# Row edges as corrections beside a convolution over all columns, and loads of X in three pairs

## The chip, the cores and the metric

The kernel runs on one core of a Trainium2 chip. The metric is device time in microseconds from the start to the end of one execution. Engines are named as the profile names them: PE multiplies matrices, PEld loads its weights, DVE and POOL work on elements, ACT scales and copies, SP issues most DMAs. Each engine works through its own queue in order and waits for the others by semaphores.

## The reference, cut to what matters

Four modulated convolutions run one after the other over rows of 1024 samples with 64 channels, for 128 batch rows, and their result is added to the input:

```python
TYPES = ('same', 'upsample', 'same', 'downsample')      # K = 3 taps, 64 -> 64 channels
def _layer(x, style, w, b, mw, mb, typ):
    s = style @ mw.T + mb
    weight = SCALE * w * s[:, None, :, None]
    demod = lax.rsqrt(jnp.sum(weight * weight, axis=(2, 3)) + EPS)
    weight = weight * demod[:, :, None, None]
    if typ == 'same':
        out = jax.vmap(_conv_same)(x, weight) + b[None, :, None]
    elif typ == 'upsample':
        out = _blur(jax.vmap(_conv_up)(x, weight.transpose(0, 2, 1, 3)) + b[None, :, None], 2.0 * blur_k, (1, 1))
    elif typ == 'downsample':
        out = jax.vmap(_conv_down)(_blur(x, blur_k, (2, 2)), weight) + b[None, :, None]
    return out
out = x
for i, typ in enumerate(TYPES):
    out = _layer(out, style, weights[i], biases[i], mod_w[i], mod_b[i], typ)
return x + out
```

Nothing in it is nonlinear in x, so away from the ends of a row the four layers are a single convolution with nine taps and a weight matrix of its own for each batch row. Near the ends, up to three outputs a side, every layer pads with zeros and cuts off what it computes beyond the row, and there the nine taps alone don't give the result.

## The kernel before, in words

The kernel works on groups of four batch rows, q = 0 to 31; two rows lie in the two halves of the 128 partitions (64 channels each), two more in a second plane. A matmul uses a 64 by 64 quadrant of PE, and four of them belong together (two halves in, two halves out). For each group a chain on PE builds the nine taps (`stage1_a`, `stage1_b`, `stage2`, `stage3_b`, `stage3_a`), while the input is turned into five sums and differences of shifted thirds of a row (`in04`, `in1`, `in2`, `in3`, `in_g01`, `in_g2`: DVE and POOL read X, write G, then T). Then five products of three matmul groups each (`conv0` to `conv4`, all in `product`, L803), over NB = 340 columns, give three interleaved planes of outputs, which ACT scales and biases into a tile `o` (`output`, L880) and SP stores (`store`, L885).

The order is written out by hand. `early_turn(q)` runs for q = 0 to 3, `turn_of(q)` for 4 to 28, and the code behind it does the last three groups. A turn finishes group q, convolves group n = q + 1, builds the taps of c = q + 2 and starts those of s = q + 4. X has two buffers. In a turn the loads of group c + 1 are issued together behind `r_sums(c)`: three planes with two DMAs each. SP issues DMAs in the order of the code, so stores and loads queue behind one another.

The ends are a second, small computation for all 128 rows at once. It takes eight input columns at each end (`x_ends` into Xe), runs all four layers on them (`ends0`, `ends1` in two parts, `ends2`, `ends3`, all through `ends_matmul`, L1044) with scalings and blurs between (`rest0` to `rest3`, `add0`, `add2`, `blur_side`), adds bias and input (`rest3_bias`) and stores three finished outputs per end (`out_ends`). Its matmul groups stand in turns 10, 14, 15 and 19 (the table SLOTS) ahead of `conv1`, in the two PSUM banks of Y, and `ends3` in turn 28 in a bank pair psE of its own. The table SIDE gives DVE one small piece of it in most turns from 8 to 27. The big convolution skips the three columns at each end, and the host puts the parts together.

Of the kernel before, what the change touches and what calls it, by code (L numbers as in the profile page):

```python
# [63 lines left out]
def kernel(  # L64
# [74 lines left out]
    Xs = [const.tile([P, 2, NXC], F32, name=f"X{i}") for i in range(NX)]  # L139
# [24 lines left out]
    Xe = const.tile([P, B, 8], F32, name="Xe")  # L164
# [9 lines left out]
    NB = 340  # L174
# [578 lines left out]
    def g_tile(q):  # L753
        if q not in Gs:
            Gs[q] = gpool.tile([P, 2, 3 * PL], F32, tag="G", name=f"G{q}")
        return Xs[q % NX], Gs[q]
# [6 lines left out]
    def in_g01(q, pairs=BOTH_PAIRS):  # L763
        if q < NQ:
            X, g = g_tile(q)
            sum_of(g[:, pairs, PL:], X[:, pairs, : 2 * PL], 0.5, X[:, pairs, PL:], ALU.subtract)
# [126 lines left out]
    WIDE = 6  # L893
    ends_ps = {}

    def slot(matmuls, n, ps, wide=WIDE):
        matmuls(ps)
        ends_ps[0] = ps, max(n, wide)

    def last(i, n, j):  # L900
        ps, w = ends_ps[0]
        return ps[i][:, : n * w].rearrange("c (b j) -> c b j", b=n)[:, :, :j]


# [81 lines left out]
    Xm = const.tile([P, B, 8], F32, name="Xm")  # L986
    Xs0 = [Xm[:, :HB], Xm[:, HB:]]
    a0, c0, a2, c2 = (const.tile([P, HB], F32, name=n) for n in ("a0", "c0", "a2", "c2"))
    g1 = const.tile([P, 6, C], F32, name="g1")

    Ye = [const.tile([P, HB, 8], F32, name=f"Ye{s}") for s in range(2)]
    Ue = [const.tile([P, HB, 11], F32, name=f"Ue{s}") for s in range(2)]
    Ve = [const.tile([P, HB, 12], F32, name=f"Ve{s}") for s in range(2)]
    Oe = const.tile([P, B, 3], F32, name="Oe")

    def zeros():
        for t in Ye:
            nc_g.memset(t[:, :, 0:1], 0.0)
            nc_g.memset(t[:, :, 7:8], 0.0)
        for t in Ue:  # L1000
            nc_g.memset(t[:, :, 0:1], 0.0)
            nc_g.memset(t[:, :, 10:11], 0.0)
        for t in Ve:
            nc_g.memset(t[:, :, 0:2], 0.0)
            nc_g.memset(t[:, :, 10:12], 0.0)
        nc_g.memset(g1, 0.0)

    def spread(t, n):

        return t[:, :, None].to_broadcast([P, t.shape[1], n])  # L1010
# [7 lines left out]
    def setup_x(h):  # L1018
        bs = slice(h * HB, (h + 1) * HB)
        nc_v.tensor_tensor(Xm[:, bs], Xe[:, bs], spread(sc[:, 0, bs], 8), op=ALU.mult)  # L1020

    def setup0():

        for rows, bs in ((T, slice(0, HB)), (Bo, slice(HB, B))):
            nc_v.tensor_mul(a0[rows], dm[rows, 1, bs], dm[rows, 0, bs])
            nc_v.tensor_copy(c0[rows], c0f[rows, bs])
# [4 lines left out]
    def setup3():  # L1031
        for rows, bs in ((T, slice(0, HB)), (Bo, slice(HB, B))):
            nc_v.tensor_copy(a2[rows], Da[rows, bs])
            nc_v.tensor_copy(c2[rows], c2f[rows, bs])

    def ends_matmul(ps, n, taps, weight, moving, wide=WIDE):
        for i in reversed(range(taps)):
            first = i == taps - 1
            w = max(n, wide)
            m = w if first else n  # L1040
            for r, rows in enumerate(HALF):
                for c, cols in enumerate(HALF):
                    dst = ps[r][cols, : HB * w].rearrange("c (b j) -> c b j", j=w)
                    nc.tensor.matmul(  # L1044
                        dst[:, :, :m],
                        weight(i, r, c)[rows],
                        moving(i, r, c, m)[rows],
                        start=first,
                        stop=(i == 0),
                        skip_group_check=True,  # L1050
                    )

    def ends0(ps):

        ends_matmul(
            ps, 6, K, lambda i, r, c: wio[0][:, i, :], lambda i, r, c, m: Xs0[c][:, :, i : i + m]
        )

    def rest0():
        for s in range(2):  # L1060
            dst = Ye[s][:, :, 1:7]
            nc_v.tensor_tensor(dst, last(s, HB, 6), spread(a0, 6), op=ALU.mult)

    def add0(s):
        dst = Ye[s][:, :, 1:7]
        nc_v.tensor_tensor(dst, dst, spread(c0, 6), op=ALU.add)

    def ends1(part):

        n = 5 - part  # L1070


        def weight(i, r, c):
            return g1[:, 2 * i + (part if c == 0 else 1 - part), :]

        def moving(i, r, c, m):
            col = 2 - i + (c + part if c else 0)
            return Ye[c][:, :, col : col + m]

        return lambda ps: ends_matmul(ps, n, K, weight, moving)  # L1080

    def rest1(part):
        n = 5 - part
        for h in range(2):
            bs = slice(h * HB, (h + 1) * HB)
            dst = Ue[h][:, :, 1 + part : 10 : 2]
            nc_v.tensor_tensor(dst, last(h, HB, n), spread(a1[:, bs], n), op=ALU.mult)

    def rest1_bias(h):

        bs = slice(h * HB, (h + 1) * HB)
        dst = Ue[h][:, :, 1:10]
        nc_v.scalar_tensor_tensor(
            dst, spread(b1s[:, bs], 9), 2.0, dst, op0=ALU.mult, op1=ALU.add
        )

    def rest1_edges(h):

        bs = slice(h * HB, (h + 1) * HB)
        for rows, col in ((T, 1), (Bo, 9)):  # L1100
            dst = Ue[h][rows, :, col]
            nc_v.scalar_tensor_tensor(
                dst, b1s[rows, bs], -0.25, dst, op0=ALU.mult, op1=ALU.add
            )

    def ends2(ps):

        ends_matmul(
            ps,
            8,  # L1110
            K,
            lambda i, r, c: wio[2][:, i, :],
            lambda i, r, c, m: Ue[c][:, :, i + r : i + r + m],
        )

    def rest2():
        for s in range(2):
            dst = Ve[s][:, :, 2:10]
            nc_v.tensor_tensor(dst, last(s, HB, 8), spread(a2, 8), op=ALU.mult)

    def add2(s):
        dst = Ve[s][:, :, 2:10]
        nc_v.tensor_tensor(dst, dst, spread(c2, 8), op=ALU.add)


    def blur_side(s, part):
        at = (2 * s, 0, 0)[part]
        src = (Ve[s], Ue[s], Ve[s])[part][:, :, at : at + 10 - part]
        dst = (Ue[s], Ve[s], Ue[s])[part][:, :, : 9 - part]
        nc_v.tensor_tensor(dst, src[:, :, :-1], src[:, :, 1:], op=ALU.add)  # L1130

    def ends3(ps):

        ends_matmul(
            ps,
            3,
            K,
            lambda i, r, c: wio[3][:, i, :],
            lambda i, r, c, m: Ue[c][:, :, i : i + 5 : 2],
            wide=3,  # L1140
        )

    def rest3():
        for h in range(2):
            bs = slice(h * HB, (h + 1) * HB)
            nc_v.scalar_tensor_tensor(
                Oe[:, bs],
                last(h, HB, 3),
                0.125,
# [572 lines left out]
```

## Time and profile before

| what | value |
|---|---|
| median of 3 runs | 475.82 us (474.04 to 476.01) |
| the profiled execution, its span | 475.5 us; no other time of it is recorded |
| DVE busy | 417.3 us |
| ACT busy | 312.0 us |
| POOL busy | 165.8 us |
| bytes read from and written to HBM | 35.36 MB, 33.62 MB |

Busy times are those of one execution, engine by engine; they overlap. In a row of the profile stand a line of the code, the engine, the operation, the tiles written and read, a form, and how often it occurred; behind it the time busy in all, the mean length of one in ns, and the idle time of the engine just before it with what ended that. Rows of the time order have start and length in us. A matmul of FP32 stands twice in the profile, once per pass.

### The profile page before, as it was taken

Reading aid. Unit: us, or ns where it says so; the run is one execution under the profiler, and the core shown is the slowest. Engines: PE = TensorE matmul, PEld = TensorE weight load, DVE = VectorE, ACT = ScalarE, POOL = GpSimd, SP = SyncE. Lnnn points to the kernel's source line nnn. Section 1 sums busy time; section 2 is a strip of 40 time slices with the busy share of each in tenths; the row PEclk is TensorE's granted clock in tenths of the full one; section 3 lists DMA queues with packets and bytes.
Section 4 is the critical chain, followed back from the end, with each engine's and each line's share of the span. In section 5 each row is a group of like instructions: output and inputs, shape, how many; then the busy total and the mean of one; then the engine's idle time right before and its main releaser. Section 6 shows DMA issues by size and latency. Waiting matters only on the chain.

```text
span 475.5 us, 26771 instructions
## 1 busy us (share of the span) xinstructions
PE 469.7 (99%) x11932; PEld 349.5 (74%) x11932; DVE 417.3 (88%) x694; ACT 312.0 (66%) x711; POOL 165.8 (35%) x200
## 2 busy tenths in 40 slices
PE   9999999999999999999999999999999999999996
PEld 6987788777678876677776677766788787876653
DVE  3889998879989998899979899979998999999896
ACT  4565657577766676766667666667666777766464
POOL 3634033664444342233432233422333423243200
PEclk9999999999999999999999999999999999999999
DMA  5237456535445554345544454543555544455225
GB/s 176 71 115 224 150 151 180 152 113 177 139 145 166 166 166 136 123 150 169 163 150 126 130 168 152 178 124 121 152 164 169 164 145 147 148 152 161 80 91 193
DMA packets 52707, 70.71 MB, mean 149 GB/s; under 512 B 6000, under 2 KB 50672, under 8 KB 52592
## 3 DMA queue, kind: packets, MB, share of 16 engines
q1 hardware_dynamic: 52368, 68.78, 46.3%
q8 instruction: 93, 1.52, 1.4%
q10 hardware_dynamic: 224, 0.22, 0.1%
q14 instruction: 22, 0.18, 0.1%
HBM read 35.36 MB, written 33.62 MB: 145 GB/s over the span
## 4 chain that ended last, share of the span: by engine, by line
PE 99%; DVE 0%; ACT 0%; issue 0%
PE psA L803 47%; PE Y L803 12%; PE psR L506 9%; PE psW L621 7%; PE psA L621 7%; PE psS L428 6%; PE psR L589 5%; PE psA L506 2%; PE Y L1044 2%; PE Y L183 1%; PE Y L379 1%; PE psM L220 0%; PE psE L1044 0%; PE Y L255 0%; DVE o L882 0%; PE psM L255 0%
## 5 line engine op out<-in xcount | busy, mean ns | idle before, releaser
L803 PE MATMUL psA<-T,H 64*64 64x340 f32 x2304 | 185.9, 446 | 0.0
L803 PEld LDWEIGHTS psA<-T,H 64*64 64x64 f32 x2304 | 90.7, 133 | 46.9 <-issue 2.5
L712 DVE SCALAR_TENSOR_TENSOR G<-X 128x1376 f32<-128x1376 f32 (+2 forms) x65 | 78.0, 1206 | 0.2
L776 POOL TENSOR_TENSOR T<-G 128x684 f32<-128x684 f32 x28 | 46.3, 1652 | 73.7 <-DVE G L712 73.7
L484 POOL TENSOR_TENSOR S<-S 128x128 f32<-128x128 f32 x28 | 21.6, 772 | 139.7 <-ACT S L399 139.6
L399 ACT ACTIVATE R<-psR,tC 128x448 f32<-128x448 f32 x63 | 36.6, 631 | 43.6 <-PE psR L506 25.8
L803 PE MATMUL psA<-T,Wf 64*64 64x340 f32 x768 | 63.7, 446 | 0.0
L803 PE MATMUL Y<-T,Wf 64*64 64x340 f32 x768 | 62.4, 451 | 0.0
L712 DVE SCALAR_TENSOR_TENSOR Y<-m,psA 128x340 f32<-128x340 f32 x62 | 32.0, 516 | 28.2 <-PE psA L803 26.9
L399 ACT ACTIVATE psW<-psA 128x128 f32<-128x128 f32 x100 | 19.3, 268 | 49.1 <-PE psA L621 45.0
L790 DVE TENSOR_TENSOR T<-G 128x1368 f32<-128x1368 f32 (+1 forms) x33 | 50.8, 1541 | 0.0
L399 ACT ACTIVATE Wf<-psW,t 128x256 f32<-128x256 f32 (+2 forms) x76 | 32.7, 480 | 26.7 <-PE psW L621 26.4
L761 DVE TENSOR_TENSOR T<-X 128x684 f32<-128x684 f32 x32 | 47.7, 1492 | 0.0
L506 PE MATMUL psR<-S,E 64*64 64x64 f32 (+1 forms) x1472 | 46.8, 237 | 0.0
L781 POOL TENSOR_TENSOR T<-G 128x684 f32<-128x684 f32 x28 | 46.5, 1660 | 0.0
L428 PEld LDWEIGHTS psS<-wd,w2n 64*64 64x64 f32 x1120 | 35.1, 133 | 12.9 <-issue 0.3
L506 PEld LDWEIGHTS psR<-S,E 64*64 64x64 f32 x1472 | 39.5, 134 | 4.9 <-ACT psR L529 0.2
L803 PEld LDWEIGHTS Y<-T,Wf 64*64 64x64 f32 x768 | 30.3, 132 | 16.8
L803 PEld LDWEIGHTS psA<-T,Wf 64*64 64x64 f32 x768 | 29.8, 133 | 14.5
L880 ACT ACTIVATE o<-psA,tb,td 128x340 f32<-128x340 f32 x63 | 37.1, 648 | 5.0 <-PE psA L803 2.8
L880 ACT ACTIVATE o<-y,tb,td 128x340 f32<-128x340 f32 x62 | 38.5, 678 | 0.0
L880 ACT ACTIVATE o<-Y,tb,td 128x340 f32<-128x340 f32 x62 | 36.1, 639 | 2.8 <-PE Y L803 2.0
(180 smaller groups left out, 840.4 us busy)
## 6 DMA issues: line engine op xcount, KB each, us to landing
out<-o SPq DMA_DIRECT2D x191, 170.0 KB, 2.6
X<-in_x SPq DMA_DIRECT2D x150, 172.0 KB, 3.4
X<-in_x SPq DMA_DIRECT2D x14, 516.0 KB, 5.0
par<-in_params SPq DMA_DIRECT2D x3, 192.0 KB, 3.8
Xe<-in_x_ends SPq DMA_DIRECT2D x1, 512.0 KB, 4.5
out<-Oe SPq DMA_DIRECT2D x2, 96.0 KB, 2.1
out<-o ACTq DMA_DIRECT2D x1, 170.0 KB, 2.8
par<-in_params SPq DMA_DIRECT2D x1, 160.0 KB, 2.7
```

Source lines behind the costliest of these rows:

```text
L399: nc_a.activation(dst, src, AF.Copy, scale=f)
L428: nc.tensor.matmul(ps[r][cols, at * C : (at + n) * C], weight[rows], wd[c if r == 0 else 1 - c][rows, taps], start=first, stop=last, skip_ ...
L506: nc.tensor.matmul(dst[r][cols], weight[rows], st[c if r == 0 else 1 - c][rows, slots, :], start=False, stop=last, skip_group_check=True,)
L589: nc.tensor.matmul(ps[r][cols, lo * C : (lo + m) * C], E[rows, e + 2, :], src[rows, a, :], start=(n == 0), stop=(n == 8), skip_group_check ...
L621: nc.tensor.matmul(dst[r][cols], weight[rows], t[rows, c, slots, :], start=first, stop=last, skip_group_check=True,)
L712: nc_v.scalar_tensor_tensor(out, x, f, y, op0=ALU.mult, op1=op)
L761: nc_v.tensor_sub(t[:, pairs, 0, :NJ], plane(X, 3, pairs), plane(X, 1, pairs))
L776: eng.tensor_add(t[:, :, 0, :NJ], plane(g, 2), plane(g, 1))
L781: eng.tensor_sub(t[:, :, 1, :NJ], plane(g, 2), plane(g, 1))
L790: nc_v.tensor_sub(t[:, pairs, :, :NJ], both(a, PL), both(b, 1))
L803: nc.tensor.matmul(ps[s][cols, :NB], w, Ts[q, tag][rows, c, i, g : g + NB], start=(g == 0 and (m == 3 or alone)), stop=(g == K - 1), skip_ ...
L880: nc_a.activation(dst, src, AF.Identity, bias=add, scale=d3)
```

## The change

Four things are changed, and they hang together.

The big convolution now computes every column: the host pads each row with four zeros instead of one, NB grows from 340 to 342, and the buffers of X and G get eight more columns, which are set to zero once for X. Outputs 0 to 1023 of a row all come out of it, the three at either end as if no layer had cut anything off.

The computation of the ends gives only what those outputs have too much. It needs three input columns per end instead of eight, and fewer columns in each layer: per end 3, then 6, 5 and 3. Both ends share tiles (a second index instead of two tiles), the right end mirrored, so that one operation serves both. `ends_matmul` now takes a plan of (weight, columns read, columns written), many of them with steps of 2 to 6 elements.

The edges are corrected on the chip. `gather(q - 1)` copies the six edge outputs of a finished group from `o` into Oc on POOL, in two small operations per turn. In turn 28 one DVE operation subtracts the corrections Oe from those of 27 groups, and one DMA stores them; the last five groups are subtracted one by one, on POOL and at the very end on DVE, and a last DMA stores them. The tables that the ends need (`end_tables`) are made on POOL in turns 8 to 10.

The places move. The end matmuls write the psA banks of the group before and stand between `stage2` and `conv2`, in turns 11, 15, 19 and 27. The loads of X are issued as three pairs: behind `r_sums`, behind the stores of the third outputs, and behind those of the second outputs.

```diff
-    Xs = [const.tile([P, 2, NXC], F32, name=f"X{i}") for i in range(NX)]
+    Xs = [const.tile([P, 2, NXC + 8], F32, name=f"X{i}") for i in range(NX)]
+    for t in Xs:
+        nc_g.memset(t[:, :, NXC:], 0.0)
...
-    NB = 340
+    NB = 342
...
+    def ends_matmul(ps, n, moving, plan):
+        for i, (weight, src, dst) in enumerate(plan):
             for r, rows in enumerate(HALF):
                 for c, cols in enumerate(HALF):
+                    out_ = ps[r][cols, : HB * n].rearrange("c (b j) -> c b j", j=n)
+                    d = dst(r) if callable(dst) else dst
                     nc.tensor.matmul(
+                        out_[:, :, d],
+                        weight(r, c)[rows],
+                        moving[rows, c, :, src],
...
     def ends0(ps):
+            Xm,
+            (
+                (w[2], slice(0, 3), slice(0, 3)),
+                (w[1], slice(0, 2), slice(1, 3)),
+                (w[0], slice(0, 1), slice(2, 3)),
+            ),
...
+    def ends1(ps):
+            Ye,
+            (
+                (g[0], slice(2, 4), slice(1, 6, 4)),
+                (g[2], slice(1, 3), slice(1, 6, 4)),
+                (g[1], slice(1, 3), slice(0, 3, 2)),
+                (g[4], slice(0, 2), slice(3, 6, 2)),
+                (g[3], slice(1, 2), slice(2, 3)),
+                (g[5], slice(0, 1), slice(4, 5)),
+            ),
...
+    def ends2(ps):
+            Ue,
+            (
+                (w[0], slice(0, 5), slice(0, 5)),
+                (w[1], slice(1, 5), slice(0, 4)),
+                (w[2], slice(2, 5, 2), slice(0, 3, 2)),
+                (w[2], slice(5, 6), slice(1, 2)),
+            ),
...
     def ends3(ps):
+            We,
+            (
+                (w[0], slice(0, 3, 2), lambda r: slice(0, 2 + r, 1 + r)),
+                (w[0], slice(4, 5), lambda r: slice(2 - r, 3 - r)),
+                (w[1], slice(1, 4, 2), lambda r: slice(0, 2 + r, 1 + r)),
+                (w[2], slice(2, 5, 2), lambda r: slice(0, 2 + r, 1 + r)),
             ),
...
+    def correct(q, planes, eng=nc_g):
+        src, b = edges(q, planes)
+        at = slice(b, b + 2)
+        if q < LATER_ENDS:
+            eng.tensor_copy(Oc[:, at, :, planes], src)
+        else:
+            eng.tensor_sub(Oc[:, at, :, planes], src, Oe[:, at, :, planes])
+
+    def gather(q):
+        for planes in (slice(1, K), slice(0, 1)):
+            correct(q, planes)
...
-    SLOTS = {
-        10: (ends0, 6, rest0),
-        14: (ends1(0), 5, lambda: rest1(0)),
-        15: (ends1(1), 4, lambda: rest1(1)),
-        19: (ends2, 8, rest2),
-    }
+    SLOTS = {10: (ends0, rest0), 14: (ends1, rest1), 18: (ends2, rest2), 26: (ends3, rest3)}
...
     def turn_of(q):
...
+            if q - 1 in SLOTS:
+                SLOTS[q - 1][0](banks(q - 1))
             conv2(q)
             r_sums(c, nc_g)
+            if q - 1 in SLOTS:
+                SLOTS[q - 1][1](A[q - 1])
             sum2(q)
             in2(n, nc_g)
         side(TABLES, q)
-        for i in range(3):
-            load(c + 1, slice(i, i + 1))
+        load(c + 1, slice(0, 1))
...
         outputs(q, 2)
+        load(c + 1, slice(1, 2))
...
         outputs(q, 1)
+        load(c + 1, slice(2, 3))
...
         outputs(q, 0)
-        if q in SLOTS:
-            matmuls, width, rest = SLOTS[q]
-            slot(matmuls, width, Y_banks)
-            rest()
-        if s == NQ:
-            slot(ends3, 3, unit(ps_w, "psE"), 3)
-            rest3()
...
         in3(c)
+        gather(q - 1)
...
+    correct(q, slice(1, K), nc_v)
     conv0(q, *range(K))
     for i, (eng, queue) in enumerate(zip(BOTH, (nc_a, nc.sync))):
         output(q, 0, i, eng)
         store(q, i, slice(0, 1), queue)
+    correct(q, slice(0, 1), nc_v)
+    store_ends(LATER_ENDS, NQ)
```

On PE, the first end convolution stood at the end of turn 10 before, between the shared taps (L506, writing psA) and `conv1` of group 11 (L803); behind it stage 2 begins (psR):

```order
L506 MATMUL psA_3057<-S_3164,E 64x64 x12
L1044 MATMUL Y<-Xm,par 64x384 x12
L803 MATMUL psA_3327<-T_11_3239,H_3059 64x340 x12
L506 MATMUL psR_0_3488<-S_3164,E 64x2x64 x2
L506 MATMUL psR_1_3489<-S_3164,E 64x2x64 x2
```

Now it stands in turn 11, between the last rows of stage 2 (psR) and `conv2` of group 11, ahead of stage 3 (L623); the third number of a form is what lies together in a step:

```order
L508 MATMUL psR_0_3508<-S_3180,E 64x64 x2
L508 MATMUL psR_1_3509<-S_3180,E 64x64 x2
L1042 MATMUL psA_3071<-Xm,par 64x192 x4
L1042 MATMUL psA_3071<-Xm,par 64x64x2 x4
L1042 MATMUL psA_3071<-Xm,par 64x64 x4
L807 MATMUL psA_3347<-T_11_3259,H_3073 64x342 x12
L623 MATMUL psA_3631<-R_3596,w0s_154 64x192 x4
```

It has moved past `conv1` and stage 2, and has three shapes of falling size where it had one.

On POOL, a turn held four operations before: a sum into S (L484), a sum into T (`in1`, L776), a sum into R (L638) and a difference into T (`in2`, L781):

```order
L484 TENSOR_TENSOR S_3164<-S_3164 128x2x64
L776 TENSOR_TENSOR T_11_3239<-G_3172 128x2x342
L638 TENSOR_TENSOR R_3301<-R_3301 128x2x128
L781 TENSOR_TENSOR T_11_3239<-G_3172 128x2x342
L484 TENSOR_TENSOR S_3434<-S_3434 128x2x64
```

Now the two copies of `gather` stand between the first two; this turn is one of the three that also make tables (c1h, Dar and c2r), at its end:

```order
L486 TENSOR_TENSOR S_3180<-S_3180 128x2x64
L1166 COPY Oc<-o_2884 128x4x2
L1166 COPY Oc<-o_2884 128x4
L780 TENSOR_TENSOR T_11_3259<-G_3188 128x2x344
L640 TENSOR_TENSOR R_3321<-R_3321 128x2x128
L785 TENSOR_TENSOR T_11_3259<-G_3188 128x2x344
L334 TENSOR_SCALAR c1h<-cc_151 64x64 x2
L1021 COPY Dar<-Da 128x128
L1022 COPY c2r<-c2f 128x128
```

So L776, now L780, has two more operations ahead of it on its engine, and the next sum into S has the tables ahead of it in turns 8 to 10.

On SP, two turns read like this before, six loads and six stores in turn:

```order
L146 DMA X_105<-in_x 128x344 x6
L885 DMA out<-o_4798 128x340 x6
L146 DMA X_106<-in_x 128x344 x6
L885 DMA out<-o_5085 128x340 x6
L146 DMA X_105<-in_x 128x344 x6
```

Now one turn and the start of the next read:

```order
L889 DMA out<-o_4833 128x342 x2
L148 DMA X_105<-in_x 128x344 x2
L889 DMA out<-o_4833 128x342 x2
L148 DMA X_105<-in_x 128x344 x2
L889 DMA out<-o_4833 128x342 x2
L148 DMA X_106<-in_x 128x344 x2
L889 DMA out<-o_5105 128x342 x2
```

The second and third pair have moved behind two and four stores of the same turn.

282 lines of the change are left out of this document (127 added, 155 removed).

## The prediction

> **What bounds the kernel now.** I read the page first, then the chain of work that ended last in order of time, then the engines' sums in one turn, then the list of waits. The page:
>
> ```profile
> span 475.5 us, 26771 instructions
> ...
> PE 469.7 (99%) x11932; PEld 349.5 (74%) x11932; DVE 417.3 (88%) x694; ACT 312.0 (66%) x711; POOL 165.8 (35%) x200
> ```
>
> PE is busy for 469.7 of 475.5 us. A busy PE need not be a fast one, so I look at what it does per turn (one pass of the loop over groups of four batch rows), in the chain that ended last (start, length, engine, tile, line) and in the sums of one turn (columns of the second fence: stretch, its length, then busy time of PE, PEld, DVE, ACT, POOL, clock, DMA share, GB/s; the first number of an engine is its time).
>
> ```profile
> 187.59 1.94 PE psR L506 x112
> 189.53 1.72 PE psA L803 x24
> ...
> 201.44 1.94 PE psR L506 x112
> ```
>
> ```profile
> 201.20:215.05 13.85, 13.85 (x388) 9.79 (x384) 12.74 (x20) 9.80 (x24) 4.81 (x4) 1.00 0.49 155
> ```
>
> The chain is PE's own work. One product (12 matmuls, 24 passes) takes 1.72 us, and stage 2 comes round again after 201.44 - 187.59 = 13.85 us, all of it PE busy at the full clock. An end convolution (L1044) is one more link: it makes its turn longer by all it costs. DVE is next with 12.74 of 13.85 us, so it has 1.11 us to spare per turn, and the waits say the same:
>
> ```profile
> DVE Y L712 <- PE psA L803: 26.9, 26, 1.9
> ```
>
> DVE waits for PE 26 times, 1.0 us each: PE sets the turn, with little room above DVE. So I price PE first, and then ask whether anything new reaches DVE's 1.1 us.
>
> **Part 1: the end convolutions that go.** Each group stands between the start of its first matmul and the start of PE's next product (PE alone, in order of time):
>
> ```profile
> 183.76 2.12 PE L1044 MATMUL Y<-Xm,par 64*64 64x384 f32 x24
> 185.70 0.74 PE L803 MATMUL psA<-T,H 64*64 64x340 f32 x6
> ```
> ```profile
> 241.06 1.92 PE L1044 MATMUL Y<-Ye,g 64*64 64x384 f32 x24
> 242.79 0.47 PE L803 MATMUL psA<-T,H 64*64 64x340 f32 x4
> ```
> ```profile
> 256.63 1.81 PE L1044 MATMUL Y<-Ye,g 64*64 64x384 f32 x24
> 258.25 0.76 PE L803 MATMUL psA<-T,H 64*64 64x340 f32 x8
> ```
> ```profile
> 313.75 2.78 PE L1044 MATMUL Y<-Ue,par 64*64 64x512 f32 x24
> 316.35 1.03 PE L803 MATMUL psA<-T,H 64*64 64x340 f32 x12
> ```
> ```profile
> 440.35 1.58 PE L1044 MATMUL psE<-Ue,par 64*64 64x192 f32 x24
> 441.75 1.04 PE L803 MATMUL psA<-T,H 64*64 64x340 f32 x12
> ```
>
> 1.94 + 1.73 + 1.62 + 2.60 + 1.40 = **9.29 us** leave PE.
>
> **Part 2: those that come.** Four quadrants run at once (24 passes of 446 ns, part 3, end in 1.72 us), so I count sets of four passes: 1.72 us / 6 sets / 340 columns = 0.843 ns a column. ends2 has the same rate (2.60 us / 6 / 512 = 0.846). The new plans hold, per quadrant, 192 + 128 + 64 = 384 columns (ends0), 4x128 + 2x64 = 640 (ends1), 320 + 256 + 128 + 64 = 768 (ends2) and 128 + 64 + 2x128 = 448 (ends3): 2240, where the old had 5184. At 0.843 ns and two passes that is 3.78 us. But most read or write every second, third or sixth element. The nearest row is ends3 of before, which reads every second element: 1.40 us / 6 / 192 = 1.215 ns, 1.44 times as much. I take 0.843 ns for the 768 columns of the matmuls that write and read runs of three or more (192, 320 and 256) and 1.215 ns for the other 1472: 1.29 + 3.58 = **4.9 us**. No row shows a write to PSUM that skips single elements. Bounds: 3.8 us if skipping is free, and 6.4 us if a skipping write costs the 1.44 once more (1.75 ns). Below 3.8 it can't go, since even dense columns take that.
>
> [...] The rows here show a skipping read, and no skipping write.
>
> **Part 3: two more columns in every product.**
>
> ```profile
> L803 PE MATMUL psA<-T,H 64*64 64x340 f32 x2304 | 185.9, 446 | 0.0
> ...
> L803 PE MATMUL psA<-T,Wf 64*64 64x340 f32 x768 | 63.7, 446 | 0.0
> L803 PE MATMUL Y<-T,Wf 64*64 64x340 f32 x768 | 62.4, 451 | 0.0
> ```
>
> 3840 passes are 160 products. Each grows by 6 sets x 2 columns x 0.843 ns = 10.1 ns, together **+1.6 us**. DVE's and ACT's rows grow by 2 in 340 as well: 12.74 us by at most 0.6% is 0.07 us of DVE's 1.11.
>
> **Part 4: the copies and corrections of the edges.** POOL now makes two small copies a turn between L484 and the sum at L776, 8 and 4 elements a partition. Small POOL operations and the idle time before L776:
>
> ```profile
> 33.69 0.23 POOL L934 TENSOR_TENSOR c2f<-sc,par_s 128x16 f32<-128x16 f32 x1
> ...
> 43.41 1.64 POOL L930 TENSOR_TENSOR Da<-sc,dm 128x16 f32<-128x16 f32 x1
> ```
> ```profile
> L776 POOL TENSOR_TENSOR T<-G 128x684 f32<-128x684 f32 x28 | 46.3, 1652 | 73.7 <-DVE G L712 73.7
> ```
>
> So a copy costs 0.23 to 1.64 us; I take 0.23, the row that is nearest in size (16 elements a partition). Two are 0.46 us, inside the 73.7 / 28 = 2.6 us that POOL sits idle there: **0**. Queued behind them is L776 (into conv1 almost a turn later). If the cover is gone, DVE pays; that is the second rival. The twelve POOL operations of end_tables in turns 8 to 10 fall in L484's idle time in the same way, and the two pads of X stand at the start, ahead of a wait.
>
> **Part 5: the new places.** The end matmuls now write psA of the turn before and stand ahead of conv2. The scaling on DVE must be done before stage 3 reopens that bank, one product (1.72 us) later; behind it on DVE stands sum2, which waits for conv2 there anyway (the 1.0 us above). So nothing is late: **0**. In turn 28 DVE gets one more operation, of 324 elements, and SP the store of its result ahead of two row stores: about 0.5 us of DVE's 1.1, **0** too. The side work on DVE shrinks (its rows have 3 to 6 elements per edge, where they had 8).
>
> **Part 6: the loads of X.**
>
> ```profile
> 211.86 0.87 DVE L712 SCALAR_TENSOR_TENSOR G<-X 128x684 f32<-128x684 f32 x1
> ...
> 212.63 1.25 ACT L880 ACTIVATE o<-y,tb,td 128x340 f32<-128x340 f32 x2
> ```
> ```profile
> DMA to landing us min/median/max: 2.4/4.2/4.4
> ```
>
> (The second fence is the landings of the loads in two turns.) The last pair now queues on SP behind the second outputs, which end at 213.9; with two issues of 0.4 us it lands by 219.2. Its first reader is the row at 211.86, one turn on: 225.7. 6.5 us to spare, so **0**; if that cover went, DVE would pay each us. Stores behind a load wait no longer than they did: a load issues at once when its buffer is free, and X's readers finish a turn earlier.
>
> **Part 7: the end.**
>
> ```profile
> 471.00 0.63 ACT L880 ACTIVATE o<-psA,tb,td 128x340 f32<-128x340 f32 x1 [2.28 <-DMA out<-o]
> 471.06 0.63 DVE L882 TENSOR_SCALAR o<-psA,td,tb 128x340 f32<-128x340 f32 x1 [0.28 <-PE psA L803]
> ```
> ```profile
> out<-o SPq DMA_DIRECT2D x191, 170.0 KB, 2.6
> ...
> out<-Oe SPq DMA_DIRECT2D x2, 96.0 KB, 2.1
> ```
>
> After the last output DVE corrects four elements (about 0.2 us) and SP issues one more store behind its own, about 0.4 us after the outputs' end at 471.7. That store is small and the last small ones landed in 2.1 us where a row store took 2.6. 0.4 - 0.5 is about nothing, 0.4 + 0.2 the worst: I take **+0.2**, between 0 and 0.6. The correction before the last DVE output fits its idle 0.28 us. The two operations of rest3_bias that go stood where DVE then waited for PE: no gain.
>
> **The sum**, against the profiled execution (475.5 us of span, 0.3 below the median 475.82 of the runs): -9.29 + 4.9 + 1.6 + 0.2 = -2.6 us. From the median: **473.2 us**. All lower bounds give -3.9 (471.9), all upper bounds -0.6 (475.2).
>
> **The rivals.**
> *Skipping writes to PSUM are dear.* Two column times (1.686 ns) for each of the 1472 columns make part 2 6.3 us and the time 474.6, no measurable change. For it: 0.37 ns more per column already for a skipping read. Against it: ends1's second half, which wrote four of every six columns, took 1.62 us where 896 columns x 2 x 0.843 ns make 1.51, hardly more.
> *The copies hold up DVE (slower).* A POOL operation can hold a DVE operation:
>
> ```profile
> 60.46 1.96 POOL L781 TENSOR_TENSOR T<-G 128x684 f32<-128x684 f32 x1
> ```
> ```profile
> 60.84 1.86 DVE L709 SCALAR_TENSOR_TENSOR Wf<-idn,t,Wf 128x64 f32<-128x64 f32 x2
> ...
> 75.75 0.47 DVE L709 SCALAR_TENSOR_TENSOR Wf<-idn,t,Wf 128x64 f32<-128x64 f32 x2
> ```
>
> The pair at L709 took 1.86 us beside a POOL sum and 0.47 without. If each copy holds in_g01 for its full length, this decides from 1.11 / 2 = 0.55 us a copy. At 0.84, halfway between the two rows' ends, it costs 1.68 - 1.11 = 0.57 us in each of 25 turns: 14 us, 487. Against it: the short row is the nearer one, and the copies stand where POOL is idle.
> *The change doesn't do what it says:* the links leave PE, but another engine fills the turns, and only parts 3 and 7 stay: 475.8 + 1.8 = 477.6. For it: DVE's 92% of a turn. Against it: the links made those five turns 1.4 to 2.6 us longer, and DVE has this on top of its 1.11 us.
>
> **How the numbers follow.** The forecast has 0.62, dear writes 0.20, held DVE 0.08, an unchanged bound 0.10. The range 471.0 to 476.6 takes in the forecast with its bounds and dear writes, and, below, half of the 1.8 us by which the lowest run (474.04) lies under the median. What a measurement of this kernel can tell from no change is 0.5%, 2.4 us: faster means below 473.4. Three quarters of the forecast's spread lies there, 0.62 x 0.75 = 0.47. Slower needs 478.2: held DVE and a little of the third, 0.09. The rest, 0.44, is within.
>
> **What would show it.** Part 1 and 2: the five L1044 groups replaced by four, of 0.8, 1.6, 1.4 and 1.1 us up to the next product (0.65 to 1.3 if skipping is free). Part 3: a product of 1.73 us, turns 13.90 apart. Part 4: copies near 0.25 us, DVE's wait for PE still near 1.0 us. Part 6: no DVE wait for a DMA. Part 7: the last packets no more than 0.6 us later after the last output. Wrong it is if DVE's waits for PE vanish, if the new groups take 1.7 ns a column, or if PE shows idle time in the turns.

## The result, and the profile after

The changed kernel takes **497.83 us** in the median (494.20 to 501.94, 4 runs) where the kernel before takes 475.04. The ratio is 1.0455, with an interval from 1.0408 to 1.0502; it leaves out the longest run, which lies more than 1.5% above the fastest. The kernel is slower, and outside the range of the prediction (471.0 to 476.6).

The page of the kernel after, with the rows in which something new stands (columns as in the tables before; q1 is the data of all DMAs, q8 is code, by the count below that of PE):

```profile
span 492.4 us, 26826 instructions
...
PE 471.3 (96%) x11948; PEld 373.0 (76%) x11948; DVE 416.0 (84%) x676; ACT 311.1 (63%) x711; POOL 177.3 (36%) x266
...
q1 hardware_dynamic: 52496, 68.65, 51.0%
q8 instruction: 93, 1.52, 1.4%
...
L623 PEld LDWEIGHTS psA<-R,w0s 64*64 64x64 f32 x1000 | 35.8, 133 | 14.3 <-issue 10.1
...
L623 PE MATMUL psA<-R,w0s 64*64 64x128 f32 (+2 forms) x1000 | 38.6, 263 | 7.6 <-issue 7.5
```

No engine has much more work: PE is busy for 471.3 us (469.7 before), DVE 416.0, ACT 311.1, and POOL's 12 us more are off the path. The span is 16.9 us longer all the same. What is new is idle time of PE in stage 3 (L623), put down to "issue": PE waited for nothing that a semaphore shows. The page of before has q1 at a smaller share for almost the same bytes:

```profile
q1 hardware_dynamic: 52368, 68.78, 46.3%
```

Two turns of the kernel after, in the columns of the turn that the prediction shows (13.85 us before):

```profile
204.30:218.45 14.15, 14.15 (x392) 10.33 (x388) 12.74 (x21) 9.78 (x24) 5.20 (x6) 1.00 0.51 147
218.45:233.50 15.05, 14.17 (x392) 11.85 (x388) 13.13 (x21) 9.92 (x24) 4.88 (x6) 1.00 0.51 139
```

In the second PE stands idle for 0.9 us at the full clock. PE in order of time in that turn:

```profile
220.55 1.91 PE L807 MATMUL psA<-T,H 64*64 64x342 f32 x24
222.28 0.65 PE L623 MATMUL psA<-R,w0s 64*64 64x192 f32 x7
223.81 0.76 PE L623 MATMUL psA<-R,w0s 64*64 64x192 f32 x17 [0.88 <-issue]
```

PE stops in the middle of a group of 24 equal matmuls, after the seventh. Missing data are an unlikely reason: the other seventeen read the same tiles, and no semaphore ends the wait. What fits is that PE lacks its own code, and the trace has a second sign of that. I numbered PE's instructions (matmuls, weight loads and those of its sequencer) and the packets of q8, which are 16,384 B each; 93 packets for some 24,000 instructions make about 258 to a packet, and the pauses show 256: PE's number grows by 768 from the pause at 355.97 us to the one at 370.29, and three packets start between them. These are six of the sixteen pauses of more than 0.35 us that fall on one place (start in us; length in ns from one matmul's start to the next; the instruction behind the pause, counted from 256 times the number of the last packet; that packet's start, how far PE then was in the same count, and data packets in flight):

```
119.34   872   449   117.93   351   15
148.13  1455   449   146.22   346   17
222.61  1199   449   221.42   416   16
298.69   475   450   296.53   345   15
370.29  1452   450   369.53   393   16
430.00  1500   450   429.27   437   19
```

All sixteen stand before instruction 449 or 450 of this count, and only pauses at this place are counted for the kernels below. As I read it, a packet has to be there when PE comes to 449. In the kernel before it starts when PE is between 165 and 338 in the count (110 to 430 us). Here it starts as late as 437, and PE goes on 2.2 to 3.5 us after the start of the packet (median 2.39), which is 1.1 to 1.6 us after its end. A turn has 772 instructions on PE (384 matmuls, 384 loads, 4 of the sequencer), three packets and four instructions, so the limit comes back in every turn a little earlier: in most turns in stage 3, just behind stage 2, whose 112 matmuls and 112 loads take 1.94 us. From 240 to 297 us, where the limits fall elsewhere in the turn, PE doesn't pause. The 256 instructions ahead of a limit in stage 3 take 3.4 to 4.0 us in most turns where PE doesn't pause (worked out from the trace of e5, below), and the packet needs 2.4 of them, so a start that is 1.0 to 1.6 us late is enough. The sixteen pauses sum to 14.3 us from start to start. The kernel before has one, of 0.4 us.

The end of the kernel has grown as well. From the lists of SP's waits, after and before (the line is that of the block around the whole kernel, and the wait stands at its end):

```profile
SPq L1727 <- DMA out<-o: 5.3, 2, 3.5
```
```profile
SPq L1713 <- DMA out<-o: 2.4, 3, 1.3
```

From the end of the last output to the end of the span pass 7.58 us (484.84 to 492.41), where 3.78 passed before (471.69 to 475.47): SP waits for a store that takes longer to be reported.

### The profile page after: what moved, and what is told of

It reads as the page before. It is cut to its first block, busy times and chain, and to the rows that moved or that the text cites. A ratio compares the mean times of both kernels' runs of the same rounds, so it can differ in the third digit from the quotient of the medians.

```text
span 492.4 us, 26826 instructions
## 1 busy us (share of the span) xinstructions
PE 471.3 (96%) x11948; PEld 373.0 (76%) x11948; DVE 416.0 (84%) x676; ACT 311.1 (63%) x711; POOL 177.3 (36%) x266
## 5 line engine op out<-in xcount | busy, mean ns | idle before, releaser
L807 PE MATMUL psA<-T,H 64*64 64x342 f32 x2304 | 190.8, 449 | 1.1 <-issue 1.1
L714 DVE SCALAR_TENSOR_TENSOR G<-X 128x1378 f32<-128x1378 f32 (+2 forms) x65 | 78.4, 1211 | 0.2
L780 POOL TENSOR_TENSOR T<-G 128x688 f32<-128x688 f32 x28 | 46.3, 1655 | 67.7 <-DVE G L714 67.7
L807 PE MATMUL psA<-T,Wf 64*64 64x342 f32 x768 | 65.0, 448 | 0.0
L807 PE MATMUL Y<-T,Wf 64*64 64x342 f32 x768 | 63.9, 450 | 1.1 <-DVE Y L714 1.1
L794 DVE TENSOR_TENSOR T<-G 128x1376 f32<-128x1376 f32 (+1 forms) x33 | 52.5, 1592 | 0.0
L763 DVE TENSOR_TENSOR T<-X 128x688 f32<-128x688 f32 x32 | 51.0, 1593 | 0.0
L785 POOL TENSOR_TENSOR T<-G 128x688 f32<-128x688 f32 x28 | 47.1, 1682 | 0.0
L623 PEld LDWEIGHTS psA<-R,w0s 64*64 64x64 f32 x1000 | 35.8, 133 | 14.3 <-issue 10.1
L623 PE MATMUL psA<-R,w0s 64*64 64x128 f32 (+2 forms) x1000 | 38.6, 263 | 7.6 <-issue 7.5
L884 ACT ACTIVATE o<-psA,tb,td 128x342 f32<-128x342 f32 x63 | 37.2, 650 | 5.0 <-PE psA L807 5.0
```

The source lines that it names most:

```text
L623: nc.tensor.matmul(dst[r][cols], weight[rows], t[rows, c, slots, :], start=first, stop=last, skip_group_check=True,)
L714: nc_v.scalar_tensor_tensor(out, x, f, y, op0=ALU.mult, op1=op)
L763: nc_v.tensor_sub(t[:, pairs, 0, :NJ], plane(X, 3, pairs), plane(X, 1, pairs))
L780: eng.tensor_add(t[:, :, 0, :NJ], plane(g, 2), plane(g, 1))
L785: eng.tensor_sub(t[:, :, 1, :NJ], plane(g, 2), plane(g, 1))
L794: nc_v.tensor_sub(t[:, pairs, :, :NJ], both(a, PL), both(b, 1))
```

## The experiments

Twelve kernels ran, in four groups. This table has what I worked out of the trace of each of them but e4: the mean length of a packet of X and of a packet of outputs (ns, between 110 and 430 us), the pauses of more than 0.35 us at the limit of a packet of code and their sum (us, from 60 us on), and the time from the end of the last output to the end of the span (us).

| kernel | time (us) | X | outputs | pauses | their sum | to the end |
|---|---|---|---|---|---|---|
| before | 475.0 to 475.6 | 76.4 | 61.7 | 1 | 0.4 | 3.78 |
| after | 497.83 | 94.2 | 65.6 | 16 | 14.3 | 7.58 |
| e1, after, loads together | 496.70 | 91.7 | 65.2 | 10 | 11.3 | 7.27 |
| e2, before, loads in pairs | 487.75 | 82.7 | 63.0 | 15 | 12.0 | 3.61 |
| e3, after, a quarter of the loads | 480.89 | - | 62.4 | 2 | 1.1 | 6.91 |
| e5, e1 with rows at 32 B | 475.13 | 73.5 | 61.7 | 1 | 0.6 | 3.52 |
| e6, before with odd rows | 484.98 | 82.3 | 62.8 | 2 | 1.8 | 6.86 |
| e7, after with rows at 32 B | 486.62 | 77.0 | 62.9 | 11 | 11.2 | 3.46 |
| e8, e1 without the copies | 494.27 | 92.8 | 64.9 | 11 | 12.1 | 7.62 |
| e9, e1, even in the array alone | 475.14 | 73.6 | 61.3 | 1 | 0.5 | 3.47 |
| e10, e1, even on the chip alone | 494.95 | 91.7 | 65.5 | 11 | 8.9 | 7.56 |
| e11, e5 with rows at 64 B | 474.89 | 73.1 | 63.2 | 0 | 0.0 | 3.56 |
| e12, e11 with a sum moved | 474.86 | 73.3 | 63.2 | 0 | 0.0 | 4.76 |

### First group: is it the place of the loads?

The theory was that the three pairs of loads put data in front of PE's code. e1 takes the pairs back in the changed kernel, e2 makes them in the kernel before, e3 loads less, and e4 takes one pair back.

e1, the changed kernel with all six loads behind R:

```diff
-        load(c + 1, slice(0, 1))
+        for i in range(3):
+            load(c + 1, slice(i, i + 1))
...
-        load(c + 1, slice(1, 2))
...
-        load(c + 1, slice(2, 3))
```

> The changed kernel with the six loads of X issued together behind R again, all else as changed. Theory A (the loads' data stands at the turn's boundary when PE asks for its next 16 KB of instructions, and the block comes late): 471.5 to 474.5 us, PE starts at L623 never more than 0.45 us apart, instruction blocks start when PE has used at most about 350 of its instructions past the last block. Theory B (the corrections on POOL and DVE hold PE through buffers; the loads are innocent): 490 to 500, as the changed kernel. Theory C (the new number of PE instructions puts the block limits in a bad place; loads innocent): 490 to 500 too.

496.70 us (494.92 to 500.25), ratio 1.045 (1.0423 to 1.0477). The theory fell in this form: without the pairs the kernel is as slow. The pauses are still there, in the list of PEld's waits of e1 and in time:

```profile
PEld psA L623 <- issue: 11.4, 16, 1.4
```
```profile
133.89 0.41 PE L623 MATMUL psA<-R,w0s 64*64 64x64 f32 x10
135.59 0.28 PE L623 MATMUL psA<-R,w0s 64*64 64x64 f32 x3 [1.29 <-issue]
```

But the packet for this limit started at 131.66, at 334 in the count, no later than in the kernel before. PE went on 3.93 us after that. Over the ten pauses of e1 the median is 4.08 us, against 2.39 in the kernel after. In the trace of the kernel before, whose loads stand in the same place, PE passes the limit without a pause as soon as 2.4 to 3.2 us after the start of the packet, in fourteen places. So the code isn't asked for late here; PE goes on late after its packet. Little of that is the packet's own transfer: PE goes on 2.56 us after the packet's end in the median of these ten pauses, and 1.33 in the kernel after. e1 also has six pauses away from the limit (at 351 to 519 in the count, 4.6 us together), put down to "issue" like the others. What PE waits for in them the trace doesn't show.

e2, the kernel before with the same three lines the other way round:

```diff
-        for i in range(3):
-            load(c + 1, slice(i, i + 1))
+        load(c + 1, slice(0, 1))
...
         outputs(q, 2)
+        load(c + 1, slice(1, 2))
...
         outputs(q, 1)
+        load(c + 1, slice(2, 3))
```

> The kernel before with its loads in three pairs at the new places, nothing else changed. Theory A: 486 to 498 us, with waits of 0.5 to 1.5 us inside stage 3 on PE that no semaphore ends. Theories B and C: 474 to 476.5, as before.

487.75 us (487.47 to 488.06), ratio 1.0254 (1.0239 to 1.0269). The pairs alone cost the kernel before 12.2 us, as the theory has it. Fifteen pauses at the limit, 12.0 us; the packets start up to 402 in the count, and PE goes on 2.35 us after their start (median). The traces show the data ahead of the code: I counted the packets of X that begin in the 2 us before a packet of code whose limit lies in stage 3 (mean between 110 and 430 us). They are 202 in the kernel after and 205 in e2, and 42 in the kernel before and 24 in e1. The packet of code itself then starts at 336 and 329 in the count, against 285 and 289.

e3, the changed kernel with its pairs, each load of turns 4 to 28 cut to its first 86 of 344 columns:

```diff
             at = slice(planes.start * PL, planes.stop * PL)
+            if part > 1:
+                at = slice(at.start, at.start + PL // part)
...
-        load(c + 1, slice(0, 1))
+        load(c + 1, slice(0, 1), part=4)
```

> The changed kernel; each load of X in turns 4 to 28 brings only the first quarter of its plane (86 of 344 columns), the rest of X stays what it was; the number, the places and the waits of the loads are unchanged. Theory A (it is the data in flight): 471 to 475 us. Theory A' (it is SP's issuing, its order or its semaphores): 488 to 500. Theory B and C: 490 to 500.

480.89 us (479.77 to 482.59), ratio 1.0113 (1.0094 to 1.0131). That is above the 471 to 475 of the theory and well below the 488 of its rival, SP's issuing. With fewer bytes in flight, and the same number, places and waits of the loads, nearly all pauses go (1.1 us are left); the long end stays (6.91 us).

e4, the changed kernel with only the third pair put back behind R:

```diff
         load(c + 1, slice(0, 1))
+        load(c + 1, slice(2, 3))
...
-        load(c + 1, slice(2, 3))
```

> The changed kernel with only the third pair of loads back behind R, next to the first; the second stays behind the third outputs. Theory A: the boundary then sees the first outputs' stores alone, as before: 471.5 to 477 us. Theories B and C: 490 to 500. If it stays above 485, it is not the third pair but the second that makes the traffic.

A ratio of 1.0576 (1.054 to 1.0611), from runs of 501.05 and 505.04 us, the slowest of all. A miss for every theory of that time, and it shows that the places of the loads don't add up one by one. Why it is slower than e1 and the kernel after isn't known.

After this group one cause was shown (the pairs, on the kernel before) and another was missing: something in e1 that isn't in the kernel before and lengthens the packets of X from 76.4 to 91.7 ns.

### Second group: the rows of the outputs

NB grew from 340 to 342. A plane of outputs is then 1368 B instead of 1360, and the planes lie one behind the other in `o` and in the output array. In the kernel before every piece begins at a multiple of 16 B; with 1368 B every second one begins 8 B past it.

e5 is e1 with the planes 344 columns (1376 B) apart in both places:

```diff
-    NB = 342
+    NB, NW = 342, 344
...
-            os[q] = opool.tile([P, 2, K, NB], F32, tag="o", name=f"o{q}")
+            os[q] = opool.tile([P, 2, K, NW], F32, tag="o", name=f"o{q}")[..., :NB]
...
-            out[q, :, s, planes.start * NB : planes.stop * NB],
-            os[q][:, s, planes].rearrange("c i j -> c (i j)"),
+            out[q, :, s].rearrange("c (i j) -> c i j", j=NW)[:, planes, :NB],
+            os[q][:, s, planes],
```

> The changed kernel with the six loads together behind R (as in the run that took 496.7 us) and the planes of the outputs 344 columns apart, on the chip side and in the output array, with 342 of them stored: every piece of 1368 B then starts at a multiple of 32 B, instead of 8 B. Theory S (the stores' new geometry makes the data DMAs longer, 76.4 to 91.7 ns for a piece of X, and PE's blocks of code come late behind them): pieces of X back near 76 ns, few stops of PE in stage 3, 472 to 477 us. Theory P (the corrections' copies on POOL and what else is new on the engines delay PE): 494 to 499 us. Theory L (the 342 columns themselves: two more in every piece and row, whatever their place): 494 to 499 us, pieces of X still at 92 ns.

475.13 us (474.23 to 475.83), ratio 0.9989 (0.9977 to 1.0). 21.6 us are gone, with the same instructions on every engine but for the places of the outputs. So neither the corrections nor the number of PE's instructions, which sets where the limits fall, can have been the cause, nor the 342 columns by themselves. The page of e5 and one of its turns:

```profile
PE 466.0 (99%) x11948; PEld 340.1 (72%) x11948; DVE 415.7 (88%) x676; ACT 311.8 (66%) x711; POOL 185.6 (39%) x266
...
q1 hardware_dynamic: 52496, 68.65, 45.2%
```
```profile
213.15:227.05 13.90, 13.90 (x392) 9.78 (x388) 12.91 (x21) 9.89 (x24) 5.20 (x6) 1.00 0.49 156
```

The turn is 13.90 us, all of it PE, and q1 has 45.2% for the bytes that took 51.0% in the kernel after.

e6 is the mirror: the kernel before, its 340 columns stored 342 apart in the array, nothing else:

```diff
-            out[q, :, s, planes.start * NB : planes.stop * NB],
-            os[q][:, s, planes].rearrange("c i j -> c (i j)"),
+            out[q, :, s].rearrange("c (i j) -> c i j", j=342)[:, planes, :NB],
+            os[q][:, s, planes],
```

> The kernel before with the planes of its 340 output columns 342 columns apart in the output array: pieces of 1360 B as before, which now start at multiples of 8 B; nothing else. Theory S: pieces of X longer than 76 ns (85 to 92), stops of PE in stage 3, 485 to 497 us. Theories P and L: 474 to 477 us.

484.98 us (483.72 to 487.72), ratio 1.0199 (1.0162 to 1.0235): 9.4 us for the place of the rows alone, with the old 1360 B. It came out at the lower edge of what was expected: 485 to 497 us, and packets of X of 85 to 92 ns, which measured 82.3. The long end is there at once (6.86 us). Few pauses at the limit pass 0.35 us (two, 1.8 us); of the 9.4 us, 3.1 stand at the end, and the rest isn't taken apart.

e7, the changed kernel with its pairs and the rows of e5:

> The changed kernel, its loads in three pairs as they are, with output planes 344 columns apart (the same edit as in the first kernel of this call). Theory S, and the pairs dear by themselves as on the kernel before (+12.2 us there): 483 to 489 us. If the pairs are dear only together with the stores' geometry: 472 to 477 us. Theories P and L: 495 to 500 us.

486.62 us (482.35 to 489.34), ratio 1.0217 (1.016 to 1.0274): the pairs cost 11.5 us here (against e5), as they do on the kernel before. The pauses of e7 are those of packets that start late (up to 433 in the count), 2.47 us from start to going on, and they have the same sign in the list of PEld's waits:

```profile
PEld psA L623 <- issue: 9.7, 10, 2.2
```

e8, e1 without the 54 copies of edges on POOL:

```diff
+        nc_g.memset(Oc, 0.0)
...
     def gather(q):
-        for planes in (slice(1, K), slice(0, 1)):
-            correct(q, planes)
+        pass
```

> The changed kernel with the six loads together behind R and without the 54 copies of output edges on POOL (turns 0 to 26; the edges of those rows come out as the uncorrected zeros less Oe). Theory P: 472 to 480 us. Theories S and L: 494 to 499 us, as with the copies.

494.27 us (493.40 to 500.38), ratio 1.0414 (1.035 to 1.0477): not to be told from e1 (1.0423 to 1.0477). The copies have no part in it that can be told.

### Third group: which side of the store, and how far

e9 is e1 with the planes 344 apart in the output array alone:

```diff
-            out[q, :, s, planes.start * NB : planes.stop * NB],
-            os[q][:, s, planes].rearrange("c i j -> c (i j)"),
+            out[q, :, s].rearrange("c (i j) -> c i j", j=344)[:, planes, :NB],
+            os[q][:, s, planes],
```

> The changed kernel with its six loads together behind R, and output planes 344 columns apart in the output array alone; on the chip they stay 342 columns (1368 B) apart. Between the run with both sides odd (496.7 us, pieces of X 91.7 ns) and the one with both even (475.1 us, 73.5 ns). If the place in the output array decides: 474 to 479 us, pieces of X 73 to 78 ns. If the place on the chip decides: 490 to 498 us. If each has a part: 480 to 489 us.

e10 is e1 with the planes 344 apart on the chip alone:

```diff
+            os[q] = opool.tile([P, 2, K, NW], F32, tag="o", name=f"o{q}")[..., :NB]
...
+            out[q, :, s].rearrange("c (i j) -> c i j", j=NB)[:, planes],
+            os[q][:, s, planes],
```

> The mirror of the kernel ahead of it: output planes 344 columns apart on the chip, 342 (1368 B) apart in the output array. The kernel before with odd rows in the output array alone took 485.0 us (+9.4) with pieces of X of 82.3 ns. If the place in the output array decides: 490 to 498 us. If the place on the chip decides: 474 to 479 us. If each has a part: 480 to 489 us, pieces of X near 82 ns.

e9 takes 475.14 us (474.25 to 476.32), ratio 0.9991 (0.9978 to 1.0005); e10 494.95 us (493.49 to 500.63), ratio 1.0427 (1.0377 to 1.0478). The place in the output array decides; the place on the chip does nothing that can be told.

e11 is e5 with the planes of X and of the outputs 352 columns (1408 B) apart in the arrays:

```diff
-    NB, NW = 342, 344
+    NB, NW = 342, 352
...
-                nc.sync.dma_start(Xs[q % NX][:, c, at], x[2 * q + c, :, at])
+                nc.sync.dma_start(
+                    Xs[q % NX][:, c, at].rearrange("c (i j) -> c i j", j=PL),
+                    x[2 * q + c].rearrange("c (i j) -> c i j", j=352)[:, planes, :PL],
+                )
```

> The version with all output pieces at multiples of 32 B (475.1 us) with the planes of X and of the outputs 352 columns (1408 B) apart in the arrays, and the outputs' planes as far apart on the chip, so that every piece starts at a multiple of 64 B in the arrays. If the step from 8 B to 32 B goes on to 64 B: pieces of X below 70 ns, the last stops of PE (1.4 us at 445 us) gone, 471.5 to 474 us. If 16 B or 32 B is all that is wanted: 474.2 to 476 us, pieces of X at 72 to 75 ns.

474.89 us (473.39 to 476.23), ratio 0.9984 (0.9969 to 0.9999). Packets of X at 73.1 ns, as in e5 (73.5): beyond multiples of 16 B (the kernel before, 76.4 ns) or 32 B (e5) nothing was gained here. The stop at 444 us stays, and this kernel has no pause at a limit, so the stop isn't one of code.

### Fourth group: what is left of the gain

In e5 PE waits once in the last turns:

```profile
444.57 0.94 PE L623 MATMUL psW<-R,w0s 64*64 64x128 f32 x24
446.61 1.96 PE L807 MATMUL Y<-T,Wf 64*64 64x342 f32 x24 [1.10 <-DVE Y L714]
```

DVE is late with Y, since the sum ahead of it took 3.03 us beside a POOL sum, and 1.59 at 435.61 (DVE and POOL of e5 in order of time):

```profile
440.77 1.86 DVE L763 TENSOR_TENSOR T<-X 128x688 f32<-128x688 f32 x1
442.55 3.03 DVE L794 TENSOR_TENSOR T<-G 128x1376 f32<-128x1376 f32 x1
445.50 1.06 DVE L714 SCALAR_TENSOR_TENSOR Y<-m,psA 128x342 f32<-128x342 f32 x2
```
```profile
441.85 2.28 POOL L785 TENSOR_TENSOR T<-G 128x688 f32<-128x688 f32 x1
```

e12 is e11 with this sum moved to a place where PE seemed not to wait for DVE:

```diff
-        if s == NQ:
-            in04(c)
         in1(c, nc_g)
...
     copy_m3(n)
+    in04(n)
     in_g01(c)
```

> The version with pieces at multiples of 64 B (474.9 us, ratio 0.9984), with one DVE sum of the last turns (T04 of the second group from the end, L794) moved from ahead of the sums into Y to behind the copy of the third product. In that version it stood there beside a POOL sum, took 3.0 us in place of 1.6, and PE waited 1.3 us for Y at 445 us, in the place where the fifth old end group (1.40 us of PE) had stood. If that wait is what gave the gain back at the end: the gap of 1.36 us ahead of the product into Y goes, 473.3 to 474.0 us, ratio near 0.995. If DVE is only late in another place instead: the gap comes up again within the next 20 us, 474.5 to 475.5 us.

474.86 us (474.21 to 476.45), ratio 0.9992 (0.9978 to 1.0006). The wait for Y is gone, and 7 us on there is another, for the next sum of DVE:

```profile
450.69 1.33 PE L810 MATMUL psA<-T,Wf 64*64 64x342 f32 x16
453.55 3.68 PE L810 MATMUL psA<-T,H 64*64 64x342 f32 x48 [1.53 <-DVE y L717]
```

DVE is busy there without a gap of note from 443.9 to 455.3 us. As I read this, DVE is the bound in the last turns, and what PE saves it waits for. A kernel with less work on DVE there wasn't tried.

## Why the prediction was wrong

**Two steps failed, and either alone takes the time out of the range. The first is part 6**, the loads of X: "6.5 us to spare, so 0". The 6.5 us are true for the readers of X; DVE waits for no load of X in the kernel after. But the step asked only who reads X, and not what else passes through the same DMA engines. The page counts PE's code there (q8, 1.4% of the 16 engines' time, beside q1 with 51.0%), and the code has some 1.0 to 1.6 us to spare at the limit behind stage 2. The pairs put data ahead of the packets (205 packets of X in the 2 us before, in e2, where there were 42): on the kernel before this costs 487.75 - 475.59 = 12.2 us (e2), on the changed one with even rows 486.62 - 475.13 = 11.5 us (e7 against e5).

**The second is part 3, which leaves a price out.** It priced the two more columns by PE's, DVE's and ACT's time, which was right, and never asked where the rows come to lie in the output array. That costs 496.70 - 475.13 = 21.6 us with the loads together (e1 against e5, and e9 against e10 for the side). In the traces it has three signs: packets of X of 92 ns instead of 74, PE still waiting for code up to 4.1 us after its packet's start (median of e1) where it passes in e5 without a pause as soon as 2.5 to 3.1 us after, and 7.3 us instead of 3.5 from the last output to the end. Of the 21.6 us of spans (494.4 and 472.8), 10.7 are pauses at the limit of a packet, 4.6 are e1's pauses away from it and 3.7 the end; the rest I haven't taken apart.

The two don't add up: 475.1 with neither, 486.6 with the pairs, 496.7 with the odd rows, 497.8 with both. The pairs make packets of code start late (after, e2, e7), and the odd rows with the loads together make PE go on late after them (e1). Why both together cost hardly more than the odd rows alone isn't shown.

The other parts, by their own steps:

*Part 1* was right: all five groups are gone from their places.

*Part 2*, 4.9 us, measured 5.24: from the start of each new group to the next product. The first and the second:

```profile
191.28 0.34 PE L1042 MATMUL psA<-Xm,par 64*64 64x192 f32 x3
...
192.11 1.32 PE L807 MATMUL psA<-T,H 64*64 64x342 f32 x13
```
```profile
249.91 0.28 PE L1042 MATMUL psA<-Ye,g 64*64 64x128 f32 x1
...
251.53 0.81 PE L807 MATMUL psA<-T,H 64*64 64x342 f32 x8
```

0.83 and 1.62, the others 1.53 and 1.26, where 0.8, 1.6, 1.4 and 1.1 were forecast. That is 1.17 ns a column over all 2240, 1.39 times the dense 0.843, and with 768 columns at 0.843 it leaves 1.34 ns for each of the other 1472. So the price lies nearer to the skipping read (1.215) than to dear writes (1.686, 6.3 us in all, an estimate that no run shows), and that rival didn't come about; reads and writes weren't measured apart.

*Part 3* was right on the engines: turns of 13.90 us where PE has its code.

*Part 4* was right. The copies took 0.23 and 0.21 us, off the path, and without them the kernel is as slow (e8):

```profile
L1166 POOL COPY Oc<-o 128x8 f32<-128x8 f32 x27 | 6.2, 231 | 0.0
L1166 POOL COPY Oc<-o 128x4 f32<-128x4 f32 x27 | 5.7, 210 | 0.0
```

DVE's waits for PE stay where they were, so DVE wasn't held, and the rival on the slower side was the wrong one:

```profile
DVE Y L714 <- PE psA L807: 29.1, 27, 2.8
```

The working of that rival had a slip: halfway between 0.23 and 1.64 us is 0.94, not 0.84, and by that it would have cost 19 us in place of 14.

*Part 5*, "nothing is late: 0", was wrong by one wait. The fifth old group (1.40 us, at 440.35) stood where DVE has no time to spare. With it gone, PE waits 1.3 us for DVE at nearly the same place (e5), and moving DVE's work only moves the wait (e12).

*Part 7* was right for the change itself, 3.52 us from the last output to the end (e5) against 3.78; the 7.58 of the kernel after belongs to the odd rows.

*The sum.* Freed of both prices the change is worth 475.13 against 475.57 us (e5), or 474.89 against 475.41 (e11): 0.1 to 0.2%, where -2.6 us were forecast. The traces of before and of e5, from stage 2 of the turn at 116 us to that at 430, differ by 311.8 - 313.5 = -1.7 us, about what parts 1 to 3 give for these turns: -7.89 + 5.24 + 22 x 0.06 = -1.3. The fifth group's 1.40 comes back as the wait, by the traces of e5 and e12. So at most some 1.7 us are left, of which the medians show 0.4 to 0.5. The profiled execution of before was a long one of its kind: its span of 475.5 us lies above the 473.1 to 473.8 of other runs that took 474.87 to 475.59 us. How the remaining us is spread isn't settled.

Of the prediction's own signs, "if PE shows idle time in the turns" was the one that came true, with a cause that none of its rivals had.

No version beats the kernel before by the 0.5% that the prediction takes for what a measurement can tell. e11 is the best, by 0.16% (0.01 to 0.31). The kernel before with its rows at 32 or 64 B wasn't tried.

## What to carry to other kernels

When rows change their width, look where each piece comes to lie in the array in memory, not only at its bytes: a pitch that keeps every piece at a multiple of 16 B or more cost nothing here, and one of 8 B cost 9 to 22 us of 475. When a transfer is moved, ask what else uses the DMA engines at that moment: here it was PE's own code (93 packets of 16,384 B), which came late behind the data, and its sign was idle time put down to nothing (pauses of up to 1.50 us), in the middle of a group of equal instructions. When a group is taken off the bounding engine, check turn by turn, the last ones too, whether the next engine has the time: here the fifth group's 1.40 us came back as a wait of PE for DVE (e5, e12).

## What the runs showed of the hardware

- PE's code came in packets of 16,384 B (q8, 93 of them), 256 instructions each by the count above. Where the packet was late, PE stopped at the same instruction of each, 449 or 450 in the count used here (sixteen times in the kernel after, fifteen in e2). PE went on 2.35 us after the packet's start in the median of e2, 2.39 in the kernel after, 2.47 in e7, and 4.08 in e1. So the late arrival came with odd rows and the loads together, and not with odd rows and the pairs; why, the traces don't show. e1 has six stops away from that instruction too (4.6 us).
- Stores whose pieces begin 8 B past a multiple of 16 B in the array lengthened the packets around them: packets of X took 91.7 instead of 73.5 ns (e1 against e5; their median stayed at 59, the slowest tenth went from 82 to over 150), while the packets of the stores themselves grew only from 61.7 to 65.2 ns. The last store was reported some 3.7 us later (7.27 us from the last output to the end in e1, 3.52 in e5). On the chip's side the same shift did nothing (e9, e10). e5 has pieces of 1368 B too, which end 8 B past a multiple of 16 B, and is fast. In e6 every second piece starts 8 B past, too, but the pieces lie 8 B apart and no two of them share 16 B; it lost 9.4 us. So the start of a piece has a price of its own. Whether pieces that meet inside 16 B cost more on top (e1 lost 21.6) wasn't tried.
- A DVE sum that takes 1.59 us at 435.61 us took 3.03 us beside a POOL sum, and that one 2.28 instead of 1.65 us (e5, at 442 us; 3.03 and 2.28 in e11 too). The DVE sum ended 1.45 us after the POOL sum did, so it made hardly any progress beside it.
